# Layer 0's attention of a two-layer model: all engines in the order of the program text, with its pieces placed anew

## The chip, the cores and the metric

The kernel runs on one NeuronCore of a Trainium2 chip. A core has five engines with instruction streams of their own: TensorE (PE: matrix products, into PSUM), VectorE (DVE), ScalarE (ACT), GpSimd (POOL) and SyncE (SP, which here only issues DMAs). An engine works its instructions off in the order in which they were built into its stream, and waits at semaphores for the others. The metric is the device time of one execution in microseconds (us); smaller is better. Of a kernel the median of several executions is given; one more execution is recorded by the profiler.

## What is computed

Input are 8 batches of 512 tokens with 512 features. Four blocks follow each other, each with a residual and a layer norm behind it: attention with 16 heads, a mixture of 8 experts of which each token takes two, a second attention, and a feed-forward layer with integer weights. The change concerns the first attention and the router behind it:

```python
x = _layernorm(x + _L0_attn_ref(x, ...))
x = _layernorm(x + _L0_ffn_ref(x, ...))
x = _layernorm(x + _L1_attn_ref(x, ...))
x = _layernorm(x + _L1_ffn_ref(x, ...))

def _L0_attn_ref(x, WQ_w, WQ_b, WK_w, WK_b, WV_w, WV_b, WO_w, WO_b):
    q = (x @ WQ_w.T + WQ_b).reshape(b, s, NH, HD).transpose(0, 2, 1, 3)    # k and v likewise
    scores = jnp.einsum('bhqd,bhkd->bhqk', q, k) * (1.0 / math.sqrt(HD))
    scores = jnp.where(causal, -jnp.inf, scores)
    attn = jax.nn.softmax(scores, axis=-1)
    out = jnp.einsum('bhqk,bhkd->bhqd', attn, v)
    return out.transpose(0, 2, 1, 3).reshape(b, s, h) @ WO_w.T + WO_b

# in _L0_ffn_ref, the choice of the experts
router_logits = xf @ gate_weight.T + xf @ gate_delta.T
probs = jax.nn.softmax(router_logits.astype(jnp.float32), axis=-1)
routing_weights, selected = jax.lax.top_k(probs, TOP_K)
```

## The kernel before

`attention0` works batch by batch (b = 0 to 7). A batch has four groups g of four heads each, and a group three units u. A unit holds one or two tiles of 128 keys: `UNITS = ((0,), (1, 3), (2,))`; because of the causal mask a tile of keys meets only the queries from it on, so that the units are 512, 384 + 128 and 256 queries wide. The text below writes (g,u) for a place in this order.

In each place `scores` computes the products of keys and queries for the four heads on TensorE into the one score buffer of PSUM (`sc`), ACT takes the exponential into `p`, and POOL sets what the mask forbids to zero. Then the thunks follow that `plan` has put at this place, and then `product`, for the unit before: the weighted sum of the values on TensorE (`av`), and on DVE the addition of `p` to the group's total. In a group's second unit `normalise` follows for the group before: TensorE sums the total over the keys (`rs`), ACT copies the sums, DVE takes the reciprocal and multiplies `av` with it into `aoT`, and POOL adds the reciprocals to a watch (`g_total`), from which the kernel tells at its end whether the numbers stayed in range.

The thunks are: the values, queries and keys of this and the next group (`value`, `query`, `key`); and for the batch before: `project` (the output projection of one of four token tiles, with the residual added on DVE; the last one calls `layernorm`, which computes statistics on DVE and the root on POOL, scales the four tiles on DVE and writes them to DRAM by four DMAs of SP's queue), `turn` (transposes of one of four feature tiles on TensorE, copied from PSUM in turns by DVE and ACT), `score` (the router's logits), and `choose` (which sorts out the two experts of each token in about 24 small DVE operations and one of ACT). For the batch before that: `dispatch` (ranks within the experts), `one_hot` (24 DVE operations) and `enter` (16 products into a table). Finally `merge` folds one low-rank correction into an expert's weights: two small products, two copies on ACT, two additions on POOL.

The products of all thunks, of `rs` and of `merge` go through two PSUM buffers (`mm`, tag "mm"); a product can start when an earlier one has left its buffer. `aoT` has one buffer, which the four projections of a batch read and `normalise` of the next batch writes anew. `xs` has two buffers, `p` has two for the first unit and one for each other.

What sets the order: up to the first batch's first place, and from group 2 of the last batch on, `in_order` holds TensorE to the order of the program text. All else, that is nearly the whole of the seven batches, and the other engines always, is put in order by a scheduler at build time. Its order is fixed in the built program. In the profile the four projections stand on TensorE in pairs and singles from (1,0) to (1,2), the four transposes in (2,1) and (2,2), in pieces between the products of `av`.

Of the kernel before, what the change touches and what calls it, by code (L numbers as in the profile page):

```python
# [18 lines left out]
P = 128  # L19
NB = 8  # L20
# [364 lines left out]
class Router:  # L385
# [76 lines left out]
    def choose(self, b, parts, ps):  # L462
# [17 lines left out]
        nc.scalar.activation(tmp, tmp, AF.Exp)  # L480
        nc.vector.tensor_reduce(red, tmp, AX.X, ALU.add)
# [640 lines left out]
def attention0(env, guard, keep, routes, experts, dram, p_mm, tiles_ctx):  # L1122
# [8 lines left out]
    with ExitStack() as phase:  # L1131
# [81 lines left out]
        def project(b, t):  # L1213
            ps = mm([P, D], "ps_o")
            for c in range(ND):
                nc.tensor.matmul(ps, lhsT=aoTs[b][:, c, ts(t, P)], rhs=wo[:, c, :], start=c == 0, stop=c == ND - 1)  # L1216
            nc.vector.tensor_tensor(xs[b][:, t, :], ps, xs[b][:, t, :], ALU.add)
            if t == NT - 1:
                env.layernorm(b, router.rows[S * b : S * (b + 1)])

        x1Ts, logits = {}, {}
# [17 lines left out]

        def choose(b):  # L1240
            router.choose(b, logits.pop(b), mm([P, NT, E], "ps_r"))
# [36 lines left out]
        def product(b, g, u, p, acc):  # L1278
# [6 lines left out]
            for kt in UNITS[u]:  # L1285
# [5 lines left out]
                at += w  # L1291
            at = 0
            for kt in UNITS[u]:
                w = S - P * kt
                if u:
                    nc.vector.tensor_tensor(total[:, :, P * kt :], total[:, :, P * kt :], p[:, :, at : at + w], ALU.add)  # L1296
                at += w

        def normalise(b, g, acc):
# [8 lines left out]
            guard.watch_inverses(r_inv)  # L1308

        merges = [(e, c) for e in range(0, E, 2) for c in range(UPS)]  # L1310
# [7 lines left out]
        def plan(b):  # L1318
# [10 lines left out]
            if b:  # L1329
                places = ((1, 0), (1, 0), (1, 1), (1, 1) if last else (1, 2))  # L1330
                for t, slot in enumerate(places):
                    todo[slot].append(lambda t=t: project(pb, t))
                places = ((2, 0),) * 4 if last else ((2, 1), (2, 1), (2, 2), (2, 2))
                for c, slot in enumerate(places):
                    todo[slot].append(lambda c=c: turn(pb, c))
                todo[(2, 1) if last else (3, 0)].append(lambda: score(pb))
                todo[(2, 2) if last else (3, 1)].append(lambda: choose(pb))
                if not last:
                    todo[2, 0].append(merge)
                    todo[3, 0].append(merge)  # L1340
            if b == 0:
                todo[1, 0].append(lambda: router.merge_lora(mm([P, ND, E], "ps_wr")))
            if b > 1:
                todo[0, 2].append(lambda: dispatch(b - 2))
                todo[1, 1].append(lambda: enter(one_hot(b - 2, range(NT))))
# [6 lines left out]

        tiles = Tiles(env, router, experts.w)
# [16 lines left out]
        begun.enter_context(in_order(tc))  # L1370
# [4 lines left out]
        for b in range(NB):  # L1375
            todo = plan(b)
            for g in range(ND):
                if g == 2:
                    if b + 1 < NB:
                        load_xT(b + 1)  # L1380

                    nc.gpsimd.tensor_tensor(xs[b], xs[b], row[:, 1:2, :].to_broadcast([P, NT, D]), ALU.add)
                if g == 3 and b + 1 < NB:
                    load_x(b + 1)
# [9 lines left out]
                for u in range(len(UNITS)):  # L1394
                    p = scores(b, g, u)
                    for thunk in todo[g, u]:
                        thunk()
                    begun.close()
                    if waiting is not None:
                        waiting()  # L1400
                    if u == 1 and summing is not None:
                        summing()
                    waiting = lambda b=b, g=g, u=u, p=p, acc=acc: product(b, g, u, p, acc)
                summing = lambda b=b, g=g, acc=acc: normalise(b, g, acc)
        waiting()
        merge(2)
        summing()
# [622 lines left out]
```

## Time and profile before

| what | us |
|---|---|
| median of 3 runs | 2297.6 |
| lowest and highest of them | 2297.3, 2299.71 |
| the profiled execution, whole | 2295.71 |
| its span, first to last instruction | 2293.9 |
| TensorE busy in the span | 2240.5 |
| DVE, ACT, POOL busy in the span | 1245.0, 648.2, 501.6 |
| start of the third value tile of batch 1 | 92.42 |
| the same in batch 2 | 183.74 |
| the same in batch 7 | 650.06 |

The mean granted clock of TensorE is 0.994 of full speed. Layer 0's attention takes about the first 720 us of the span. "Busy" is the union of an engine's records. Matmuls overlap each other and their ends are modelled, so that a busy TensorE can also be one that waits between two of them. TensorE's waits in the first 740 us, as far as the profile shows them as idle time, are few:

```profile
PE sc L1264 <- ACT p L1268: 5.2, 7, 1.8
PE ps_q L1200 <- DMA experts<-in_xT: 4.4, 1, 4.4
PE ps_v L1193 <- DVE v L1195: 2.4, 4, 1.0
```

In such a line the instruction that waited stands first, behind the arrow the one that released it, then the total, the number of waits and the longest.

### The profile page before, as it was taken

The numbers are of one execution on the slowest core, as the hardware profiler recorded it, in microseconds if no ns is written. First come the engines' busy times: TensorE is split into PE (matmuls) and PEld (weight loads), VectorE is DVE, ScalarE is ACT, GpSimd is POOL, SyncE is SP. The second block draws the span as 40 slices with busy tenths as digits, with TensorE's granted clock in tenths as the row PEclk, the third lists the DMA queues.
The fourth block names the chain that finished last, engine by engine and source line by source line (L and its number), as shares of the span: only waits on it lengthen the run. The fifth ranks groups of instructions, "written<-read, shape, count | busy, mean of one in ns | idle before, by whom it ended". The sixth has DMA issues, their size and how long they took to land.

```text
span 2293.9 us, 24187 instructions
## 1 busy us (share of the span) xinstructions
PE 2240.5 (98%) x9430; PEld 1154.8 (50%) x9430; DVE 1245.0 (54%) x1974; ACT 648.2 (28%) x937; POOL 501.6 (22%) x493
## 2 busy tenths in 40 slices
PE   9999999999999999999998999999998999999997
PEld 3344444444444444444443334443343878888876
DVE  3457575666668432242216877777667544444443
ACT  2332323323324221111223323333332322222222
POOL 2231323413224231131125122321211000000000
PEclk9999999999999999999999999999999999999999
DMA  8010110101112234332233011100100100000000
GB/s 289 19 56 1 55 33 23 56 7 49 54 38 84 92 115 146 93 120 91 87 127 94 10 55 56 55 29 17 37 1 23 42 19 19 19 19 19 19 19 20
DMA packets 58444, 126.63 MB, mean 55 GB/s; under 512 B 6210, under 2 KB 6210, under 8 KB 58322
## 3 DMA queue, kind: packets, MB, share of 16 engines
q1 hardware_dynamic: 47040, 89.32, 11.1%
q0 software_dynamic: 10560, 34.61, 5.2%
q8 instruction: 77, 1.26, 0.2%
q10 hardware_dynamic: 722, 1.07, 0.1%
q14 instruction: 45, 0.37, 0.1%
HBM read 89.59 MB, written 35.39 MB: 54 GB/s over the span
## 4 chain that ended last, share of the span: by engine, by line
PE 76%; issue 8%; DVE 7%; DMA 4%; POOL 4%; ACT 2%; POOLq 0%; SPq 0%; ACTq 0%; DVEq 0%
PE ps_f L1069 7%; PE ps_g L1055 6%; PE ps_u L1055 6%; PE ps_gu L845 5%; PE ps_o L1216 5%; PE ps_o L1551 5%; PE av L1601 5%; PE sc L1579 4%; PE ps_q L1503 4%; PE ps_q L1200 4%; PE ps_k L1208 4%; PE ps_v L1193 4%; PE av L1288 3%; PE sc L1264 3%; PE ps_y L862 2%
## 5 line engine op out<-in xcount | busy, mean ns | idle before, releaser
L845 PE MATMUL ps_gu<-experts,xrT 128*128 128x512 f32 (+1 forms) x520 | 248.6, 601 | 0.0
L1268 ACT ACTIVATE p<-sc 128x2048 f32<-128x2048 f32 (+1 forms) x96 | 152.9, 1593 | 189.0 <-PE sc L1264 182.1
L1273 POOL TENSOR_SCALAR_AFFINE_SELECT p<-p 128x512 f32<-128x512 f32 x128 | 92.1, 734 | 380.1 <-ACT p L1268 376.6
L1060 DVE SCALAR_TENSOR_TENSOR hT<-ps_u,vec,sg 128x512 f32<-128x512 f32 x88 | 65.8, 748 | 201.4 <-PE ps_u L1055 201.4
L1069 PE MATMUL ps_f<-ffn_w,h_half 128*128 128x512 f32 x672 | 169.4, 392 | 1.1 <-DVE h_half L1064 1.1
L934 POOL TENSOR_TENSOR g_total<-g_total,r_inv 128x512 f32<-128x512 f32 x64 | 89.7, 1402 | 361.4 <-DVE r_inv L1612 286.2
L1612 DVE RECIPROCAL r_inv<-r_inv 128x512 f32<-128x512 f32 x32 | 106.8, 3339 | 105.4 <-ACT r_inv L931 105.4
L1582 ACT ACTIVATE p<-sc 128x1024 f32<-128x1024 f32 x128 | 124.1, 1021 | 130.3 <-PE sc L1579 119.7
L1296 DVE TENSOR_TENSOR p<-p 128x1536 f32<-128x1536 f32 (+2 forms) x96 | 129.3, 1346 | 38.5 <-POOL p L1273 21.5
L1055 PE MATMUL ps_g<-x_high,ffn_w 128*128 128x512 f32 x352 | 141.5, 402 | 3.0 <-DVE x L1557 3.0
L1069 PEld LDWEIGHTS ps_f<-ffn_w,h_half 128*128 128x128 f32 x672 | 124.5, 188 | 33.7 <-DVE h_half L1064 7.2
L848 DVE TENSOR_TENSOR h<-ps_gu,h 128x256 f32<-128x256 f32 x67 | 28.4, 424 | 205.2 <-ACT h L847 205.2
L1055 PE MATMUL ps_g<-x_low,ffn_w 128*128 128x512 f32 x352 | 139.4, 396 | 0.0
L1055 PE MATMUL ps_u<-x_high,ffn_w 128*128 128x512 f32 x352 | 139.2, 395 | 0.0
L1055 PE MATMUL ps_u<-x_low,ffn_w 128*128 128x512 f32 x352 | 139.2, 395 | 0.0
L1579 PE MATMUL sc<-qT,kT 64*128 64x512 f32 x512 | 127.9, 618 | 1.0 <-ACT qT L1505 0.7
L862 PE MATMUL ps_y<-experts,hT 128*128 128x512 f32 (+1 forms) x272 | 127.9, 592 | 0.5 <-ACT hT L856 0.5
L1200 PE MATMUL ps_q<-experts 128*128 128x512 f32 x256 | 120.4, 611 | 4.4 <-DMA experts<-in_xT 4.4
L845 PEld LDWEIGHTS ps_gu<-experts,xrT 128*128 128x128 f32 x520 | 89.6, 192 | 68.0 <-issue 68.0
L1601 PE MATMUL av<-p,v 128*64 128x512 f32 x512 | 123.8, 605 | 0.0
L1193 PE MATMUL ps_v<-experts 128*128 128x512 f32 x256 | 116.3, 602 | 2.4 <-DVE v L1195 2.4
L1208 PE MATMUL ps_k<-experts 128*128 128x512 f32 x256 | 117.5, 602 | 0.2 <-ACT r_inv L931 0.2
(256 smaller groups left out, 3544.5 us busy)
## 6 DMA issues: line engine op xcount, KB each, us to landing
results<-y SPq DMA_DIRECT2D x68, 256.0 KB
x<-in_x SPq DMA_DIRECT2D x8, 1024.0 KB
experts<-in_gate_up SPq DMA_DIRECT2D x8, 1024.0 KB
rows<-x SPq DMA_DIRECT2D x32, 256.0 KB
x<-rows SPq DMA_DIRECT2D x8, 1024.0 KB
experts<-in_xT SPq DMA_DIRECT2D x7, 1024.0 KB
out<-x SPq DMA_DIRECT2D x28, 256.0 KB
ffn_i<-in_wq_ffn SPq DMA_DIRECT2D x11, 512.0 KB
```

The costliest lines, as they stand in the source:

```text
L845: mm = nc.tensor.matmul(ps, lhsT=xT[:, c, :], rhs=self.weights(i, c), start=c == 0, stop=c == ND - 1)
L862: self.nc.tensor.matmul(ps, lhsT=hT[:, c, :], rhs=self.weights(i, ND + c), start=c == 0, stop=c == self.NI - 1)
L1055: nc.tensor.matmul(ps, lhsT=w[:, ts(dc, P)], rhs=x[:, dc, :], start=(dc, i) == (0, 0), stop=(dc, i) == (ND - 1, 1))
L1069: self.nc.tensor.matmul(os[t], lhsT=h[:, ts(t, P)], rhs=self.weights(2 * NHID + c), start=(c, i) == (0, 0), stop=(c, i) == (NHID - 1, 1))
L1193: nc.tensor.matmul(ps, lhsT=xts[b][:, c, ts(t, P)], rhs=wv[:, c, :], start=c == 0, stop=c == ND - 1)
L1200: nc.tensor.matmul(ps, lhsT=wq[:, g, ts(c, P)], rhs=xts[b][:, c, :], start=c == 0, stop=c == ND - 1)
L1208: nc.tensor.matmul(ps, lhsT=wk[:, g, ts(c, P)], rhs=xts[b][:, c, :], start=c == 0, stop=c == ND - 1)
L1268: nc.scalar.activation(p, sc[:, :, :width], AF.Exp, scale=scale)
L1296: nc.vector.tensor_tensor(total[:, :, P * kt :], total[:, :, P * kt :], p[:, :, at : at + w], ALU.add)
L1579: nc.tensor.matmul(sc[:, j, :], lhsT=st["kT"][hs, ts(kt, P)], rhs=st["qT"][g][hs, :], start=True, stop=True)
L1582: nc.scalar.activation(p, sc, AF.Exp, scale=scale)
L1601: nc.tensor.matmul(st["av"][HD * j : HD * (j + 1), :], lhsT=st["v"][:, kt, HD * j : HD * (j + 1)], rhs=p[:, j, :], start=kt == 0, stop=kt ...
```

## The change

Three things change, for batches 0 to 6. The in-order stretch now starts at the same place, but covers DVE, ACT and POOL as well as TensorE, and lasts to the start of the last batch. The pieces of the batch before are placed anew: projections at (1,0), (1,1), (1,2) and (2,0), ahead of the other thunks there; the layer norm cut into statistics beside each projection and a scaling step `norm` at (2,2); all four transposes at (3,0), the logits at (3,1), the choice's first half at (3,2) and its second half at (0,0) of the next batch; the one-hots in two halves at (1,2) and (2,0), and their entry into the table at (2,2). The bias is added to `xs` in four pieces from (2,0) to (3,0), and the next batch's `x` is loaded at (3,1). And in every place the addition to the total is cut off from `product` and stands ahead of the thunks, as do the watches of the reciprocals.

Batch 7 keeps its places, except for the second half of batch 5's choice, the additions and the watches; its order is the scheduler's up to group 2, as before.

```diff
@@ class Router, choose
         nc.vector.tensor_tensor(tmp, ps, bc(red), ALU.subtract)
         nc.scalar.activation(tmp, tmp, AF.Exp)
+
+        yield
         nc.vector.tensor_reduce(red, tmp, AX.X, ALU.add)
@@ project
             nc.vector.tensor_tensor(xs[b][:, t, :], ps, xs[b][:, t, :], ALU.add)
+            if b >= NB - 2:
+                if t == NT - 1:
+                    env.layernorm(b, router.rows[S * b : S * (b + 1)])
+                return
+            if t == 0:
+                norms[b] = [small.tile([P, NT, n], F32, name=name) for n, name in ((6, "stats"), (2, "mv"), (1, "rstd"))]
+            stats, mv, rstd = norms[b]
+            nc.vector.bn_stats(out=stats[:, t, :], in_=xs[b][:, t, :])
+            nc.vector.bn_aggr(out=mv[:, t, :], in_=stats[:, t, :])
             if t == NT - 1:
-                env.layernorm(b, router.rows[S * b : S * (b + 1)])
-
+                nc.gpsimd.tensor_scalar(rstd[:, :, 0], mv[:, :, 1], LN_EPS, None, ALU.add)
+                nc.gpsimd.tensor_tensor(rstd[:, :, 0], rstd[:, :, 0], env.neg_half, ALU.pow)
+
+        def norm(b):
+            stats, mv, rstd = norms.pop(b)
+            for t in range(NT):
+                x = xs[b][:, t, :]
+                nc.vector.tensor_scalar(x, x, mv[:, t, 0:1], rstd[:, t, :], ALU.subtract, ALU.mult)
+                nc.sync.dma_start(out=router.rows[S * b + P * t : S * b + P * (t + 1)], in_=x)
...
+        def begin_choice(b):
+            choosing[b] = router.choose(b, logits.pop(b), mm([P, NT, E], "ps_r"))
+            next(choosing[b])
+
+        def end_choice(b):
+            next(choosing.pop(b), None)
@@ product, now without the additions
+
+        def add(u, p, acc):
+            total, _ = acc
             at = 0
             for kt in UNITS[u]:
                 w = S - P * kt
-                if u:
-                    nc.vector.tensor_tensor(total[:, :, P * kt :], total[:, :, P * kt :], p[:, :, at : at + w], ALU.add)
+                nc.vector.tensor_tensor(total[:, :, P * kt :], total[:, :, P * kt :], p[:, :, at : at + w], ALU.add)
                 at += w
@@ plan
             if b:
-                places = ((1, 0), (1, 0), (1, 1), (1, 1) if last else (1, 2))
+                places = ((1, 0), (1, 0), (1, 1), (1, 1)) if last else ((1, 0), (1, 1), (1, 2), (2, 0))
                 for t, slot in enumerate(places):
-                    todo[slot].append(lambda t=t: project(pb, t))
...
+                    todo[slot].insert(0, lambda t=t: project(pb, t)) if not last else todo[slot].append(lambda t=t: project(pb, t))
...
+            elif b:
+                todo[2, 2].insert(0, lambda: norm(pb))
+                todo[3, 0] += [lambda c=c: turn(pb, c) for c in range(ND)]
+                todo[3, 1].append(lambda: score(pb))
+                todo[3, 2].append(lambda: begin_choice(pb))
+                todo[2, 0].append(merge)
+                todo[3, 0].append(merge)
+
+            for t, slot in enumerate(((2, 0), (2, 1), (2, 2), (3, 0))):
+                todo[slot].append(lambda t=t: nc.gpsimd.tensor_tensor(xs[b][:, t, :], xs[b][:, t, :], row[:, 1, :], ALU.add))
+            if b + 1 < NB:
+
+                todo[3, 1].append(lambda: load_x(b + 1))
...
             if b > 1:
+                todo[0, 0].append(lambda: end_choice(b - 2))
                 todo[0, 2].append(lambda: dispatch(b - 2))
-                todo[1, 1].append(lambda: enter(one_hot(b - 2, range(NT))))
+                if last:
+                    todo[1, 1].append(lambda: enter(one_hot(b - 2, range(NT))))
+                else:
+                    todo[1, 2].append(lambda: one_hot(b - 2, (0, 1)))
+                    todo[2, 0].append(lambda: rows.append(one_hot(b - 2, (2, 3))))
+                    todo[2, 2].append(lambda: enter(rows.pop()))
@@ the loop
-        begun.enter_context(in_order(tc))
+        begun.enter_context(in_order(tc, mybir.EngineType.DVE, mybir.EngineType.Activation, mybir.EngineType.Pool))
         query(0, 0)
         key(0, 0)
...
         for b in range(NB):
+            if b == NB - 1:
+                begun.close()
...
                     p = scores(b, g, u)
+                    while watches:
+                        guard.watch_inverses(watches.pop())
+                    if waiting is not None and waiting[2]:
+                        add(*waiting[2:])
                     for thunk in todo[g, u]:
                         thunk()
-                    begun.close()
                     if waiting is not None:
-                        waiting()
+                        product(*waiting)
                     if u == 1 and summing is not None:
-                        summing()
-                    waiting = lambda b=b, g=g, u=u, p=p, acc=acc: product(b, g, u, p, acc)
-                summing = lambda b=b, g=g, acc=acc: normalise(b, g, acc)
+                        normalise(*summing)
+                    waiting = b, g, u, p, acc
+                summing = b, g, acc
```

## The prediction

> **What bounds the kernel now.** I read the table by stretches first, with one stretch for each batch of layer 0's attention from batch 1 on. Columns: length; busy time and instructions of TensorE (PE), its weight loads, DVE, ACT and POOL; granted clock; DMA share; GB/s.
>
> ```profile
> 361.00:454.00 93.00, 92.13 (x477) 39.41 (x476) 59.40 (x112) 28.14 (x32) 28.93 (x27) 1.00 0.10 35
> 454.00:548.00 94.00, 92.42 (x477) 39.72 (x478) 60.88 (x112) 28.30 (x33) 28.93 (x27) 1.00 0.10 34
> ```
>
> TensorE is busy 98% of a batch, at full clock; DVE is busy 59 to 61 of 93 us. Next, TensorE's timeline of batch 5.
>
> ```profile
> 506.34 3.60 PE L1216 MATMUL ps_o<-experts,aoT 128*128 128x512 f32 x8
> ...
> 514.00 1.15 PE L1264 MATMUL sc<-q,k 32*128 32x384 f32 x16 [0.57 <-ACT p L1268]
> 515.08 3.70 PE L1200 MATMUL ps_q<-experts 128*128 128x512 f32 x8
> 518.62 0.60 PE L1228 MATMUL ps_x1T<-ident,x 128*128 128x128 f32 x4
> 519.15 1.04 PE L1288 MATMUL av<-p,v 128*32 128x512 f32 x2
> 520.12 0.66 PE L1228 MATMUL ps_x1T<-ident,x 128*128 128x128 f32 x4
> 520.71 0.63 PE L1288 MATMUL av<-p,v 128*32 128x512 f32 x3
> ```
>
> Busy time hides waits here: two records of the av product take 1.04 us in line 519.15, eight of them in unbroken form take 0.88 (500.30 to 501.18). So I count by start to start of unbroken pieces: a tile of v, q, k or o 3.53 (16 a batch); scores of the three units 1.07, 1.08, 0.65; av 0.88, 1.00, 0.57; row sums 0.97 (all seven four times); rank 0.46, table 1.84, a turn 0.53 (4), logits 1.00, a merge's pair 0.96 (2), router 0.89. The sum is 89.6 us. The third v tile starts at 183.74 in batch 2 and at 650.06 in batch 7: 93.3 a batch. So 3.7 us a batch are waits and broken pieces, and about 22 over batches 1 to 6: all that a better order could win.
>
> Third, DVE's timeline of the same batch.
>
> ```profile
> 503.18 3.35 DVE L1306 RECIPROCAL r_inv<-r_inv 128x512 f32<-128x512 f32 x1
> 506.44 2.83 DVE L1296 TENSOR_TENSOR p<-p 128x512 f32<-128x512 f32 x2
> 509.97 0.69 DVE L1307 TENSOR_TENSOR aoT<-av,r_inv 128x512 f32<-128x512 f32 x1 [0.70 <-PE ps_o L1216]
> 510.58 0.68 DVE L1217 TENSOR_TENSOR x<-ps_o,x 128x512 f32<-128x512 f32 x1
> ```
>
> The first group's normalising product writes aoT, of which there is one buffer; so it waits for the last projection of the batch before (506.34 to 509.86 on TensorE). Here the wait costs little: adds are put in front of it, and it waits 0.70 us.
>
> **The change, part by part.** I write (g,u) for group g, unit u, and follow a batch from 2 to 6. Its program holds DVE, ACT and POOL to written order as well.
>
> *Gains.* TensorE's pieces stand unbroken: the 3.7 us go, as far as nothing new waits.
>
> *Products, adds, watches, the choice's second half.* The counts stay. The score sums' adds stand ahead of a unit's own DVE work, and what they wait for (POOL's masking of a unit earlier) is long done. The choice's 24 small operations take about 6 us in (0,0) (456.0 to 462.9 before, adds among them); TensorE meanwhile computes scores and two tiles, over 8 us, so nothing waits. In (0,2) the rank product needs the last v's eviction, behind an add of 2.23 us: 0.3. The four POOL adds of the bias (4.65 us as one) lie beside TensorE. DMA issues do not change in count; on SP's queue x's load moves from the start of group 3 to (3,1) and the norm's four row writes from (2,1) (514.26) to (2,2), and x is wanted first in the next batch's (2,0), 40 us later: nothing. Cover gone, the load's 7.5 us (528.72) would show.
>
> *First new stall, (1,1) to (2,0).* The fourth projection moves from (1,2) to (2,0), but the aoT product stands in (1,1), and it waits for that projection. DVE runs in order, so behind it stand the add of (1,2), the third projection's eviction, its statistics and half of the one-hots (12 operations, 2.4). DVE's reciprocal is over some 9 us before the projection; DVE stands still. When the projection ends, TensorE wants the merge's two PSUM tiles; the first takes the buffer of the third projection. DVE must do: the product 0.60, add 1.68 + 0.55, eviction 0.70, and two hand-overs of 0.1 to 0.15: 3.8 us of waiting. The second tile uses the first's buffer and waits for ACT's copy, 0.60 and two hand-overs: 0.8. Together 4.6.
>
> POOL's rstd (0.32 + 1.04) waits for the fourth projection's statistics; behind it queue the merge's adds (2.83), a bias add (1.2) and the masks of (2,1) (1.23), 6.6 us in all. DVE's add of (2,2) wants these masks some 7.7 us after the statistics (the other half of the one-hots, the query, reciprocal and product lie between): nothing, with 1 us to spare; without it the norm below is later by as much.
>
> *Second new stall, (3,0).* The norm's four operations now stand in (2,2) behind reciprocal, product and add; the transposes follow at once in (3,0). From the end of (2,1)'s row sums: reciprocal starts after 1.05 (49.58 to 50.63 in batch 0), then 3.26 + 0.60 + 2.23 + 4 × 1.03 = 11.3 us to the last norm. TensorE arrives after 0.65 + 3.53 + 1.84 + 1.00 + 1.07 = 8.1; three of four transposes of the first turn are hidden, so 2.9. The second turn's buffer is the table's, two DVE operations (0.46, 0.42) later: 0.7. The third waits for the first's copy, behind an add (1.15 + 0.68 after the table, less what TensorE did): 1.3. The merge waits for the third's copy beyond the fourth turn: 0.4. Together 5.3. The before kernel spread the turns over (2,1) and (2,2).
>
> A batch so becomes 89.6 + 0.3 + 4.6 + 5.3 = 99.8, or +6.5; five batches: +32.5. Batch 1 has no table and no one-hots: 87.3 of work; its second merge tile waits for the fourth projection's eviction (0.93 + 1.15 + 0.70 after the third's; 6.2 in all), and its transposes arrive 1.84 earlier (6.2 in all): 99.7 against 91.3 before (92.42 to 183.74), +8.4. In batch 0 nothing stands between the first unit's scores and the second's but an av of 0.57 (0.88 more once), while exp takes 1.88 and two hand-overs: 1.4 + 1.4 + 0.6 of waiting, less about 1.3 that the broken queries and a POOL wait cost before: +2.1. Stalls: +43.
>
> *The clock.* Each of these stretches leaves TensorE nearly empty for 5 to 8 us. The trace shows what follows. Columns: stretch, length, TensorE busy, clock, DMA.
>
> ```profile
> 1216.00:1218.00 2.00, 0.00 (x0) 1.00 0.00 0
> 1220.00:1222.00 2.00, 1.91 (x5) 0.50 0.03 8
> 1222.00:1224.00 2.00, 2.00 (x8) 0.65 0.00 0
> 1224.00:1226.00 2.00, 2.00 (x8) 1.00 0.00 0
> ```
>
> After a gap of 4.87 us (1215.22 to 1220.09) TensorE runs about 3.4 us at half clock, which loses 1.7 us of work. After one of 3.00 (1775.25) it drops too (0.56 at 1778 to 1780), and after 1.76 + 0.54 (0.50 at 722 to 724). The price is bounded below by 0 a stretch (work that waits anyway loses nothing) and above by two such periods, 3.4. I take 1.7, since both stretches hold more idle time than the three in the trace that tripped or come near the longest: 12 stretches in batches 1 to 6, +20.
>
> The Trainium skill ("TensorE: Matmul & The Clock Gate", Part 1) speaks against such an order: a whole idle window of about 3.4 us halves the clock until a busy window has passed. By that rule a gap of 3.8 us holds a free-running whole window only at times, so by an estimate from the page the first stretch would trip perhaps half the time, and the sum would be some 5 us less. The trace dropped after 1.76 + 0.54, so the sum stays with the trace.
>
> Sum: +43 + 20 = +63. The profiled execution's span of 2293.9 (run 2295.7) becomes 2357 (2359). Its run lies 1.9 below the median of 2297.6, so the median becomes 2361.
>
> **The rivals.**
> *Stalls alone, the clock holds.* The merges and turns inside the stretches may count as activity: 699 to 702 lost 0.44 + 0.94 without a drop. Against it: the three drops above. 2297.6 + 43 = 2341.
> *Worse.* POOL's watch and bias adds run beside DVE; the 1024-wide add took 2.10 instead of 1.21 beside POOL's watch (507.18), the 1536-wide 2.17 instead of 1.76 (543.99). In (3,0) that is 0.4 + 0.9, over six batches 8; and a second period of half clock at each stretch adds up to 20. 2361 + 8 + about 12 = 2381.
> *Faster.* If the aoT product found its buffer free and the norm came in time, all of the 22 us would be won: 2297.6 - 22 = 2276. For it speaks TensorE's broken timeline; against it the wait in the line at 509.97, and the written order behind it. This decides if the two stretches cost together under 3.7 us instead of 9.9.
> *The order is not kept,* and waits stay as they were: 2298. The built program's order of all engines is the written one up to batch 6, and TensorE's order from batch 7 on is that of before, so I give it little.
>
> **How the numbers follow.** Stalls and clock, 2361: 0.56. Stalls alone, 2341: 0.22. Worse, 2381: 0.14. Faster, 2276: 0.05. No change: 0.03. Low end: the stalls alone less 20% of their 43 us, 2333. High end: the worse case and a little, 2386; outside lie the faster and unchanged cases and the ends of the others, about 0.18. Within 0.2% (4.6 us, about what a measurement of this kernel can tell) lies only the last case: same 0.03, faster 0.05, slower 0.92.
>
> **What would show it.** In the changed profile, among TensorE's waits: the merge's lora tiles for DVE's eviction of ps_o, about 3.8 us each, six times; the transposes for the norm, about 3; the aoT product on DVE waiting for ps_o some 9 us. DVE's busy time should not change by more than a few us. A stretch of one batch should last 100 to 104 us; a clock of 0.97 or so in it shows the drops, 1.00 that there are none. The prediction is wrong if TensorE finds the merge's buffer free at the end of the fourth projection, if the norm ends before the table does, or if DVE's order turns out to differ; batches of 90 us would be the faster rival's.

## The result, and the profile after

The changed kernel takes 2397.3 us (median of four runs, 2395.7 to 2399.7) beside 2297.5 of the kernel before on the same chip: a ratio of 1.0439, 95% interval 1.0418 to 1.0461. The forecast was 2361 with a range to 2386: the direction was right, the size was not. The profiled execution has a span of 2393.6 us, 99.7 more than before.

First, where the time lies. Lines of the code are those of the changed kernel from here on (the aoT product is L1339, the fourth projection's matmuls L1218, its eviction L1219, the norm L1237, the turns L1248, the adds L1328, the merge's pair L751). Start to start of the first value tile, batches 2 to 6 now last 109.8, 109.4, 109.0, 109.4 and 109.3 us, where they lasted 92.8 to 93.9. Batch 1 lasts 17.3 more than before, batch 0 2.7 more, and what follows the start of batch 7 takes 1652.8 us against 1652.6. So the whole loss lies in batches 0 to 6. The stretches of two batches, in the columns of the prediction's first lines (length; TensorE, its weight loads, DVE, ACT, POOL; granted clock; DMA):

```profile
413.00:522.00 109.00, 100.05 (x480) 42.24 (x476) 63.09 (x112) 28.59 (x32) 27.86 (x30) 0.92 0.09 30
522.00:631.00 109.00, 100.41 (x479) 42.48 (x476) 62.70 (x112) 28.59 (x32) 27.86 (x30) 0.91 0.09 29
```

Two things changed at once. TensorE's busy share fell from 98 to 92%, that is 8.6 us of waits a batch. And its busy time rose by 8 us with the same instructions, because the granted clock fell from 1.00 to 0.91. DVE, ACT and POOL are busy as long as before, within 4 us.

What TensorE waited for in batches 0 to 6, up to 740 us (total, times, longest):

```profile
PE ps_lora L751 <- DVE x L1219: 23.7, 7, 3.8
PE ps_x1T L1248 <- DVE x L1237: 12.1, 11, 3.3
PE ps_rank L517 <- DVE v L1197: 4.6, 5, 0.9
...
PE ps_x1T L1248 <- DVE x1T L162: 4.1, 6, 1.0
PE ps_lora L751 <- ACT scaled L762: 3.7, 5, 0.7
```

These are the two stretches of the prediction by name: the merge's tile for the third projection's eviction, six times 3.85 us, and the transposes for the norm. DVE's side of the first one, in batch 5:

```profile
566.12 3.35 DVE L1338 RECIPROCAL r_inv<-r_inv 128x512 f32<-128x512 f32 x1 [1.85 <-ACT r_inv L933]
578.78 0.69 DVE L1339 TENSOR_TENSOR aoT<-av,r_inv 128x512 f32<-128x512 f32 x1 [9.31 <-PE ps_o L1218]
579.38 2.54 DVE L1328 TENSOR_TENSOR p<-p 128x1536 f32<-128x1536 f32 x2
581.85 0.69 DVE L1219 TENSOR_TENSOR x<-ps_o,x 128x512 f32<-128x512 f32 x1
```

DVE stands still for 9.31 us at the head of its queue, waiting for the fourth projection; then come, in order, the product, the add and the eviction that TensorE wants. This is the forecast's chain, at its forecast length (3.85 us against 3.8).

TensorE's timeline through both stretches shows what the forecast did not have:

```profile
575.04 3.70 PE L1218 MATMUL ps_o<-experts,aoT 128*128 128x512 f32 x8
582.59 2.07 PE L751 MATMUL ps_lora<-lora 16*128 16x512 f32 x2 [3.85 <-DVE x L1219]
585.40 2.07 PE L751 MATMUL ps_lora<-lora 16*128 16x512 f32 x2 [0.75 <-ACT scaled L762]
587.40 1.08 PE L1318 MATMUL av<-p,v 128*32 128x256 f32 x8
588.41 2.09 PE L1294 MATMUL sc<-q,k 32*128 32x384 f32 x16
...
605.70 1.24 PE L1248 MATMUL ps_x1T<-ident,x 128*128 128x128 f32 x3 [1.26 <-DVE x L1237]
607.43 0.33 PE L1248 MATMUL ps_x1T<-ident,x 128*128 128x128 f32 x1 [0.49 <-DVE x L1237]
608.22 1.11 PE L1248 MATMUL ps_x1T<-ident,x 128*128 128x128 f32 x4 [0.46 <-DVE r_table L560]
609.95 1.97 PE L1248 MATMUL ps_x1T<-ident,x 128*128 128x128 f32 x8 [0.62 <-DVE x1T L162]
611.85 2.81 PE L751 MATMUL ps_lora<-lora 16*128 16x512 f32 x4
```

Eight records of av with 256 columns take 1.08 us at 587.40 and 0.64 elsewhere (529.17); the scores of 384 columns 2.09 instead of 1.15. TensorE runs at half speed well after the wait is over. To see how long, I cut the time at the points where the clock changes (length, TensorE busy, clock, DMA):

```profile
577.53:580.94 3.41, 1.21 (x3) 1.00 0.00 0
580.94:584.36 3.42, 1.77 (x2) 0.50 0.00 0
584.36:587.77 3.41, 2.66 (x7) 0.50 0.01 2
587.77:591.18 3.41, 3.41 (x25) 0.50 0.00 0
591.18:594.59 3.41, 3.41 (x12) 1.00 0.00 0
```

and in the second stretch:

```profile
604.83:608.24 3.41, 1.34 (x5) 1.00 0.64 235
608.24:611.65 3.41, 2.79 (x12) 0.50 0.31 116
611.65:615.07 3.42, 3.42 (x14) 0.50 0.50 139
615.07:618.48 3.41, 3.41 (x25) 0.50 0.43 168
618.48:621.89 3.41, 3.41 (x12) 1.00 0.00 0
```

Each of these two periods of half clock lasts three windows of 3.41 us, 10.24 us, where the forecast had one. Over the whole attention there are 12 such periods, one for each stretch as forecast: ten of three windows, one of four (in batch 1) and one of two (in batch 4), together 122.9 us or 36 windows. Half of what TensorE was busy in them is work lost: 53.6 us (the forecast's term was 20). In the window from 611.65 TensorE was busy all of the time, and the clock stayed at half all the same.

### The profile page after: what moved, and what is told of

Its sections match the earlier page's. It is cut to its first block, busy times and chain, and to the rows that moved or that the text cites. A ratio compares the mean times of both kernels' runs of the same rounds, so it can differ in the third digit from the quotient of the medians.

```text
span 2393.6 us, 24209 instructions
## 1 busy us (share of the span) xinstructions
PE 2292.4 (96%) x9430; PEld 1171.2 (49%) x9430; DVE 1261.3 (53%) x1974; ACT 650.4 (27%) x937; POOL 499.9 (21%) x517
## 3 DMA queue, kind: packets, MB, share of 16 engines
q8 instruction: 77, 1.26, 0.2%
## 4 chain that ended last, share of the span: by engine, by line
PE 77%; DVE 9%; issue 7%; DMA 2%; POOL 2%; ACT 2%; POOLq 0%; DVEq 0%; ACTq 0%; SPq 0%
PE ps_f L1071 6%; PE ps_g L1057 6%; PE ps_u L1057 6%; PE ps_q L1202 5%; PE ps_gu L847 5%; PE ps_o L1218 5%; PE av L1653 5%; PE ps_o L1603 5%; PE sc L1631 4%; PE ps_q L1555 4%; PE ps_v L1195 4%; PE sc L1294 4%; PE av L1318 3%; PE ps_k L1210 3%; DVE p L1328 3%
## 5 line engine op out<-in xcount | busy, mean ns | idle before, releaser
L1303 POOL TENSOR_SCALAR_AFFINE_SELECT p<-p 128x512 f32<-128x512 f32 x128 | 85.0, 676 | 429.6 <-ACT p L1298 420.1
L1664 DVE RECIPROCAL r_inv<-r_inv 128x512 f32<-128x512 f32 x32 | 106.8, 3339 | 106.6 <-ACT r_inv L933 106.6
L936 POOL TENSOR_TENSOR g_total<-g_total,r_inv 128x512 f32<-128x512 f32 x64 | 82.4, 1287 | 350.8 <-DVE r_inv L1664 287.4
L1328 DVE TENSOR_TENSOR p<-p 128x1536 f32<-128x1536 f32 (+2 forms) x96 | 137.2, 1429 | 5.1 <-PE av L1318 1.9
L1338 DVE RECIPROCAL r_inv<-r_inv 128x512 f32<-128x512 f32 x32 | 107.3, 3352 | 56.0 <-ACT r_inv L933 55.9
L1555 PE MATMUL ps_q<-hT,attn_qkv 128*128 128x512 f32 x256 | 117.6, 602 | 0.0
```

The source lines that it names most:

```text
L1555: nc.tensor.matmul(ps, lhsT=w_qkv[:, c, ts(g, P)], rhs=hT[:, c, :], start=c == 0, stop=c == ND - 1)
```

## The experiments

Fourteen kernels, each against the kernel before on the same chip (1.00 is the kernel before). "Half" is the sum of half-clock windows up to 760 us, worked out as above. In the faster runs this takes in the start of batch 7: of the sums of runs 5 and 7 to 14 some 4 to 14 us lie there, as do the 6.8 of the kernel before.

| run | what it is | us | ratio, 95% interval | half, us | work lost, us |
|---|---|---|---|---|---|
| before | the kernel before | 2297.5 | 1 | 6.8 | 3.3 |
| after | the change | 2397.3 | 1.0439 (1.0418 to 1.0461) | 122.9 | 53.6 |
| 1 | projections early | 2355.7 | 1.0258 (1.0221 to 1.0295) | 61.4 | 28.5 |
| 2 | norm early | 2373.2 | 1.0334 (1.0312 to 1.0357) | 71.7 | 32.1 |
| 3 | both | 2348.2 | 1.0225 (1.0208 to 1.0243) | 41.0 | 20.3 |
| 4 | 128-row merge | 2380.9 | 1.0368 (1.0346 to 1.0390) | 85.3 | 35.4 |
| 5 | only TensorE in order | 2313.9 | 1.0073 (1.0050 to 1.0095) | 35.3 | 17.3 |
| 6 | before, all in order | 2396.4 | 1.0430 (1.0401 to 1.0460) | 95.6 | 29.2 |
| 7 | all in order, spread | 2327.3 | 1.0130 (1.0101 to 1.0158) | 54.6 | 27.1 |
| 8 | 7, merge in (3,2) | 2339.6 | 1.0183 (1.0161 to 1.0204) | 44.4 | 19.3 |
| 9 | TensorE in order, turns spread | 2313.3 | 1.0076 (1.0049 to 1.0103) | 23.2 | 11.4 |
| 10 | all in order, turns spread | 2317.2 | 1.0098 (1.0071 to 1.0126) | 34.1 | 17.0 |
| 11 | only DVE free | 2313.2 | 1.0081 (1.0053 to 1.0109) | 33.6 | 16.4 |
| 12 | 9, choice earlier | 2303.2 | 1.0025 (1.0016 to 1.0034) | 17.1 | 8.5 |
| 13 | 12, choice earlier still | 2311.7 | 1.0070 (1.0054 to 1.0086) | 23.9 | 11.2 |
| 14 | 7 with 128-row merge | 2313.8 | 1.0073 (1.0055 to 1.0091) | 17.1 | 7.5 |

### Runs 1 to 3: each stretch taken away

Run 1:

```diff
-                places = ((1, 0), (1, 0), (1, 1), (1, 1)) if last else ((1, 0), (1, 1), (1, 2), (2, 0))
+                places = ((1, 0), (1, 0), (1, 1), (1, 1)) if last else ((1, 0), (1, 0), (1, 1), (1, 1))
-                for t, slot in enumerate(places):
+                for t, slot in reversed(list(enumerate(places))) if not last else enumerate(places):
```

> Here all four projections stand in (1,0) and (1,1), two in each, so the fourth is over before the first group's normalising product; nothing else differs from the changed kernel. Theory (a stretch costs its idle time and then three windows of 3.41 us at half clock): the first stretch goes in batches 1 to 6 with 3.85 + 0.75 us of waits and the 3.2 to 4.4 us of work that the half clock lost there (23.5 in all), so 51 us less: about 2346, one period of half clock a batch left, of about 10.2 us. Rival A (the waits alone matter, the clock's share lies elsewhere): 28 less, 2370. Rival B (the wait moves: some other DVE work becomes late for TensorE in (1,0) to (2,0)): no more than 15 less.

Run 2:

```diff
-                todo[2, 2].insert(0, lambda: norm(pb))
+                todo[2, 1].insert(0, lambda: norm(pb))
```

> The norm moves from the front of (2,2) to the front of (2,1), ahead of that unit's reciprocal; the fourth projection stays in (2,0). Theory: the transposes of (3,0) find their rows ready, the waits for the norm (about 1.8 a batch) go, those for the table's eviction and for x1T's copy (1.1) may stay; if the idle time left is too short to halve the clock, the period of half clock at (3,0) goes too (29.9 in all): 40 to 45 us less, about 2355. Rival A (the short waits that are left still halve the clock): 11 less, 2386. Rival B (the norm's four operations make DVE late for the next thing in (2,1) or (2,2)): unchanged, 2397, or more.

Run 3 has both edits.

> Both edits of the two kernels before. Theory: both stretches go; the clock stays at 1.00 through batches 1 to 6; of the 109.4 us of a batch 8.6 and about 7 go, 93 to 94 are left, and the time is 2298 to 2310, about that of the kernel before; if the broken pieces of the kernel before are also won, as much as 2280. Rival (one of the waits only moves): 2340 or more.

Run 1 came 41.6 us below the changed kernel (its two times are 2349.8, which is the profiled one, and 2361.7). The merge's 3.85 us are gone from the waits and the six periods at (2,0) with them, worth more than the 28 of waits alone (rival A). But 9 us of the forecast 51 did not come. That is less than the two times lie apart, but the trace shows that rival B has a part in it: TensorE's row sums now wait 2.7 us in each of five batches for a score sum's add. One-hots stand in front of that add on DVE, and TensorE, no longer held up before them, arrives while they run.

Run 2 came 24 us below, between the theory (40 to 45) and rival A (11). The waits for the norm are gone; the period at (3,0) stayed in batch 1, vanished in 2 and 3 and is one window in 4 to 6. But a new wait of up to 1.7 us for the query's eviction (behind the norm) appeared in five batches, 6.4 us in all, as rival B had it, and that for the copies of the turns rose from 4.1 to 9.1. The first stretch, which the edit leaves as it was, halved the clock for three windows in batches 1 to 3 and for two in batches 4 to 6: where the windows happen to begin also decides how many of them a gap costs.

Run 3 is the telling miss: 2348, the rival's side, not 2300. Both stretches are gone, and batches 2 to 6 still last 102.4 us each. From 458 to 562 us of run 3, a batch and a little more:

```profile
PE ps_k L1210 <- DVE q L1204: 6.0, 2, 3.0
PE rs L1335 <- DVE p L1328: 2.7, 1, 2.7
PE ps_rank L517 <- DVE v L1197: 0.9, 1, 0.9
```

The first two of these waits are not among the changed kernel's. DVE's timeline of run 3 shows the first one's making: twelve one-hots (from 453.30) and the norm (455.61, 1.91 us) stand ahead of the query's eviction at 457.44, for which TensorE's key tile waited 3.0 us. Moving one thing in a strictly ordered queue makes the next thing late.

### Runs 5, 6 and 11: whose order is it

Run 5, and run 11 with Activation and Pool kept in the list:

```diff
-        begun.enter_context(in_order(tc, mybir.EngineType.DVE, mybir.EngineType.Activation, mybir.EngineType.Pool))
+        begun.enter_context(in_order(tc))
```

> The changed kernel's places and steps, with TensorE alone held to the written order; DVE, ACT and POOL are ordered by the scheduler again. In the program so built TensorE's instructions stand exactly as in the changed kernel; on DVE the adds and the third projection's eviction stand ahead of the first group's normalising product, and the norm stands right behind the fourth projection's statistics, in (2,0). Theory (both stretches come from DVE's written order, and the half clock from the stretches): waits of 4.6 and 3 us and their 12 periods of half clock go, 2290, between 2275 and 2310, a clock of 1.00 in most of batches 2 to 6. Rival (the new places or TensorE's unbroken order cost by themselves, whatever DVE does): 2340 or more.

> The changed kernel with its places; only DVE is ordered by the scheduler again, TensorE, ACT and POOL stay in written order. Theory (the stretches are DVE's doing alone): as with all three free, 2314 within 8. Rival (POOL's written order, in which rstd stands behind the masks, or ACT's, makes up a part): 2335 or more.

Run 6 is the other half of the change: the kernel before, its places and steps unchanged, with all four engines in written order up to the last batch.

> The kernel before, places and all, with TensorE, DVE, ACT and POOL held to written order in batches 0 to 6. Theory (the written order puts DVE's work late where a wait stands at the head of its queue): the product still stands ahead of the fourth projection's eviction and now the whole norm and the adds stand behind it; slower than before by 2 to 5%, 2340 to 2400, with periods of half clock in each batch. Rival (only the moves of the fourth projection, the norm and the turns hurt, the written order alone wins the broken pieces): 2275 to 2300.

Run 5 came 4 us above its theory's range, and of batches 1 to 6 only 4 and 6 kept the full clock; runs 6 and 11 came out inside theirs. On the cause the three agree. With the changed kernel's places, and TensorE's instructions in exactly its order, freeing the other three engines brings 2313.9, and freeing DVE alone brings the same 2313.2: ACT's and POOL's written order costs nothing that can be measured. The written order on the old places costs 2396.4, as much as the whole change. So, at the new places, 83 of the 100 us are DVE's written order, and the places and steps with TensorE's order cost the other 16. Of these 16 some 14 are the half clock again (17.3 us of lost work in run 5, 3.3 in the kernel before). A reader of run 6 finds other waits than in the changed kernel, but the same kind:

```profile
PE ps_x1T L1228 <- DVE x L153: 25.8, 24, 2.1
PE ps_x1T L1228 <- DVE q L1202: 23.5, 6, 3.9
PE ps_table L556 <- DVE one_hot L547: 17.4, 40, 1.4
```

Run 5 also shows whether unbroken pieces win anything. Its batches without any half clock, 4 and 6 (all engines, as above):

```profile
371.50:464.60 93.10, 91.97 (x480) 39.09 (x476) 56.80 (x109) 28.52 (x32) 27.51 (x29) 1.00 0.10 35
562.70:655.90 93.20, 92.07 (x481) 39.15 (x477) 55.65 (x108) 28.52 (x32) 27.53 (x29) 1.00 0.12 34
```

TensorE's pieces are unbroken there, its waits are 1.1 us, and a batch lasts 93.2 us: what it lasted before. The 3.7 us a batch that the forecast booked as won are not there.

### Runs 4 and 14: what holds the clock down

```diff
     def merge(self, e, c, ps, scaled, factors=None):
...
-            self.delta(ps[i], e + i, c)
+            if factors:
+                self.nc.tensor.matmul(ps[i], lhsT=factors[0], rhs=factors[1], start=True, stop=True)
+            else:
+                self.delta(ps[i], e + i, c)
```

with factors = (wo[:, 0, :P], wo[:, 0, :]) in all 24 merges, twelve in batches 1 to 6 and twelve between 820 and 950 us: 128 rows instead of 16, the same 512 columns. The kernel so leaves out the low-rank corrections. Run 4 does this to the changed kernel, run 14 to run 7.

> The changed kernel, with the merge's matmuls of the low-rank factors (16 rows x 512) replaced by matmuls of the same size in columns with 128 rows (a tile of the output projection's weights by itself): as long, as many, same waits. It leaves out the factors, so the experts' weights of the first two groups come out as others. Theory A (a window counts as busy by how much of the array works, and 16 rows of 128 count for little, so that the merge's pairs hold the clock down): the period of half clock at (3,0) lasts two windows (6.8 us) instead of three, that of (2,0) two or three; 1.7 us less for each window, 10 to 20 us less in all: 2377 to 2387. Theory B (only idle time counts, any matmul is work): periods as long as before, 2397 within 3.

TensorE's waits in run 4 are those of the changed kernel (24.1 us for the eviction, 12.1 for the norm, 3.7 for ACT's copy), and yet the time is 16.4 us less; in the profiled executions 13.6 us of the gain lie in batches 0 to 6 and 2.1 behind them. The half-clock windows fell from 36 to 25, the lost work from 53.6 to 35.4. That is theory A's number, and it prices the clock apart from the waits. The second stretch lost windows in every batch (19 in all to 11), the first only some (17 to 14). The second stretch of run 4 in batch 5, cut where the clock changes:

```profile
593.65:597.07 3.42, 1.90 (x11) 1.00 0.65 251
597.07:600.48 3.41, 2.00 (x8) 0.50 0.72 264
600.48:603.89 3.41, 3.41 (x11) 0.50 0.17 27
603.89:607.31 3.42, 3.42 (x29) 1.00 0.76 284
```

The third window holds the last transposes (1.5 us) and the merge (1.9 us) and nothing idle, and after it the clock is back. In batch 4 of run 4 the windows begin at nearly the same point of the stretch as in the changed kernel's batch 5:

```profile
491.26:494.67 3.41, 2.72 (x12) 0.50 0.33 125
494.67:498.09 3.42, 3.42 (x5) 0.50 0.45 147
498.09:501.50 3.41, 3.41 (x29) 1.00 0.41 160
```

The first of these, with twelve records of transposes, is the changed kernel's window at 608.24; the second, a transpose and then the merge, is the one at 611.65. There the clock stayed at half, here it came back, so it is not only a matter of where the windows begin. In the first stretch the rows alone are not enough: run 4's window from 467.36, with the second pair of the merge in it, was busy for 2.67 of 3.42 us, like the one at 584.36, and both stayed at half. There the second wait (0.75 us) has its part. In run 7 a window with the same contents, transposes 1.3 and a 16-row merge 2.1, does not bring it back, nor does the next:

```profile
547.71:551.12 3.41, 1.58 (x14) 1.00 0.21 79
551.12:554.54 3.42, 3.42 (x12) 0.50 0.02 8
554.54:557.95 3.41, 3.41 (x25) 0.50 0.79 299
557.95:561.36 3.41, 3.41 (x12) 0.50 0.00 0
```

So a window in which TensorE's records leave no gap is not always a busy one to the clock: with 16 rows of 128 it stayed at half, with 128 rows it rose. That the clock weighs rows is what fits; the runs show only these two sizes. It fits the drops too, here in run 5 and then in run 3:

```profile
519.86:523.28 3.42, 3.09 (x17) 1.00 0.00 0
523.28:526.69 3.41, 3.41 (x18) 0.50 0.00 0
```

```profile
452.30:455.72 3.42, 1.71 (x16) 1.00 0.00 0
455.72:459.13 3.41, 0.89 (x2) 1.00 0.63 235
```

The window of run 5 is busy for 3.09 us, of which the two 16-row pairs of a merge fill 2.2, and the clock drops behind it. The first window of run 3 is busy for 1.71 us with row sums and scores alone, and the clock stays.

> The seventh run's places (the one with two projections each in (1,0) and (1,1), one-hots there, the norm in (2,0), all engines in written order; 2327), with the merge's 16-row matmuls replaced by 128-row ones as in the fourth run. It leaves out the factors. In batches 4 to 6 of the seventh run the clock is halved for three windows although TensorE is never idle in them. Theory A (rows count): the periods shrink to one window or none, of 27 us of lost work 12 to 20 go, about 2310. Theory B (only idle time or the transposes count): the periods stay, 2327 within 4.

Run 14 came 13.5 us below run 7, with the half-clock periods of batches 3 to 6 gone altogether. That is on theory A's side, but it says less than run 4: the windows of a run lie on a fixed grid (below), and in run 14 a line of the grid (546.39) falls into the second of the two waits at the turns (to 545.41 and to 547.14), which lie in one window in run 7. A part of the gain can be that, and 3.6 us of it lie behind batch 6.

### Runs 7 to 10, 12 and 13: a better order

Run 7:

```diff
...              (the places of the projections as in run 1)
-                    todo[1, 2].append(lambda: one_hot(b - 2, (0, 1)))
-                    todo[2, 0].append(lambda: rows.append(one_hot(b - 2, (2, 3))))
+                    todo[1, 0].append(lambda: one_hot(b - 2, (0, 1)))
+                    todo[1, 1].append(lambda: rows.append(one_hot(b - 2, (2, 3))))
-                todo[2, 2].insert(0, lambda: norm(pb))
+                todo[2, 0].append(lambda: norm(pb))
```

> All engines in written order; as in the third run two projections each in (1,0) and (1,1), and besides, the two halves of the one-hots in (1,0) and (1,1), where DVE stood idle, and the norm at the end of (2,0). Theory: of the waits of the third run those of the row sums for the score sums' add (2.7 a batch) and of the key for the query's eviction (3.0) go, with the period of half clock behind them (1.7); the small waits and the period of half clock at the turns and the merge in (3,0) stay (1.7): 7.4 less in each of five batches, about 2311. Rival (the norm in (2,0) makes the row sums wait as the one-hots did): 2325 to 2345.

Run 8 is run 7 with the second merge moved:

```diff
-                todo[3, 0].append(merge)
+                todo[3, 2].append(merge)
```

> As the kernel before it in this set, with the merge of (3,0) moved to (3,2), away from the turns. Theory (a window of transposes and 16-row matmuls counts as idle, even with little idle time in it): without the merge the windows at (3,0) hold enough full matmuls, the last period of half clock goes, 1.7 a batch: 10 less than the kernel with the merge in (3,0), about 2300. Rival (idle time alone decides): the same as that kernel, within 3.

Run 7's waits came out as expected (row sums gone, the key's at 0.2), but it took 2327 instead of 2311: the period at the turns grew from one window to three in batches 4 to 6, 98.9 us a batch, for the reason seen above. Run 8 was a miss: the merge in (3,2) meets the choice's PSUM tile and waits for DVE's reading of it, 14.0 us in six batches. Its time can't test what it was made for. In its trace the period at the turns is gone in batches 2 to 6, as its theory has it, but there too a line of the grid (560.15) falls between the two waits at the turns (to 559.75 and to 561.48), so that the merge need not be the reason.

Runs 9 and 10 take run 7's places, the table to (1,2) and the turns away from the merge; run 9 with TensorE alone in order, run 10 with all engines. The lines are those of run 9; in run 10 the turns stand in (2,1), (2,2), (2,2) and (3,0):

```diff
-                todo[3, 0] += [lambda c=c: turn(pb, c) for c in range(ND)]
+                for c, slot in enumerate(((2, 1), (2, 1), (2, 2), (2, 2))):
+                    todo[slot].append(lambda c=c: turn(pb, c))
-                    todo[2, 2].append(lambda: enter(rows.pop()))
+                    todo[1, 2].append(lambda: enter(rows.pop()))
```

> TensorE alone in written order, DVE, ACT and POOL ordered by the scheduler, as in the fifth run; besides, two projections each in (1,0) and (1,1), the one-hots there too, the table in (1,2), the norm in (2,0), two turns each in (2,1) and (2,2), each pair behind eight or more full matmuls; merges stay in (2,0) and (3,0). Theory (windows with many transposes and 16-row matmuls halve the clock, and the fifth run's 17.3 us of work lost to it is all that keeps it above the kernel before): at most two periods of half clock are left, 2285 to 2300. Rival (the turns now wait for PSUM buffers in (2,1) and (2,2) as the kernel before did): 2305 to 2320.

> All engines in written order, projections, one-hots, table and norm as in the run beside it, the turns one in (2,1), two in (2,2), one in (3,0). Theory: the two stretches are gone and the turns no longer stand beside the merge, so the 27 us of work that the fourth set of places lost to the half clock go for the most part: 2300 to 2312. Rival (DVE's written order makes the turns' copies wait behind reciprocal and adds, and TensorE with them): 2330 or more.

Run 9 missed its theory: the periods at the turns are gone, but the second value tile now waits 2.3 to 2.6 us for DVE to read the choice's tile, which the scheduler put behind the reciprocal, and one window at half clock follows in most batches. Run 10 came out 5 us above its theory's range, and 80 us below the changed kernel with all four engines in written order as well. So it is not the written order as such that costs 83 us, but the places that stood in it.

Run 12 is run 9 with the logits moved to the front of (3,1) and the choice's product to its end (the lines below). Run 13 puts the logits at the end of (3,0) and the whole choice, no longer cut in two, at the front of (3,1), and holds TensorE to the written order from batch 1 on only:

```diff
-                todo[3, 1].append(lambda: score(pb))
-                todo[3, 2].append(lambda: begin_choice(pb))
+                todo[3, 1].insert(0, lambda: score(pb))
+                todo[3, 1].append(lambda: begin_choice(pb))
```

> As the ninth run (TensorE alone in written order, projections, one-hots, table, norm and turns moved), with the logits at the front of (3,1) and the router's product at its end, ahead of the row sums, instead of in (3,2). On DVE the two operations that read the product's PSUM tile then stand ahead of the add and the reciprocal. Theory (the ninth run's wait of the second value tile, 2.3 to 2.6 a batch, and the period of half clock behind it, 1.7, are all that lie between its 96 us a batch and 92): about 20 less than it, 2290 to 2296, at or a little under the kernel before. Rival (a batch's work in this order is no shorter than the 93.3 us of the kernel before, whatever waits): 2298 or more.

> As the twelfth run, with the logits at the end of (3,0), the whole choice at the front of (3,1), and TensorE's written order from batch 1 on only (batch 0 is the scheduler's, as before). Theory (the wait of the third value tile for the first's eviction, 1.4 to 1.8 a batch, goes, and batch 0 wins back its 2.7 us): 10 to 12 us less than 2303, 2290 to 2293, and a batch of 91.5 to 92. Rival (93 us is what a batch's TensorE work takes in any order): 2298 to 2301.

Run 12 is the best of all at 2303.2, and still 0.25% (0.16 to 0.34%) slower than the kernel before: the rival. Its batches 3 to 5 last 93.2, 93.9 and 92.9 us; it loses 2.7 us in batch 0 and about 2 each in batches 2 and 6 (95.7 and 95.4). Run 13 came out above both its theory and its rival, 8.6 us slower than run 12: the logits wait 1.4 us for ACT's copy of the merge, the key 1.5 for the query's eviction, and a window of half clock follows in most batches. No version beat the kernel before; the shortest of batches 2 to 6 in any of them lasts 92.9 us, in the kernel before 92.8.

## Why the prediction was wrong

Step by step, by its own terms, in us for one batch of 2 to 6 (after: batch 5, 522.11 to 631.52; its lost work is 3.92 + 4.81):

| term | predicted | measured | worked out |
|---|---|---|---|
| bare TensorE work | 89.6 | 92.1 | 100.82 busy less 8.73 lost to the clock |
| rank | 0.3 | 0.9 | wait for the value tile's eviction |
| first stretch | 4.6 | 4.6 | 3.85 + 0.75 |
| second stretch | 5.3 | 2.8 | 1.26 + 0.49 + 0.46 + 0.62; 0.8 more lies in the transposes' records |
| clock | 3.4 | 8.7 | 3.92 + 4.81 |
| batch | 103.2 | 109.4 | with 0.3 of small gaps |

*The step that failed is the clock term, "I take 1.7".* That each of the twelve stretches would trip the clock was right, twelve of twelve. Its price was mis-sized: 4.5 us of work on the mean (53.6 / 12) instead of 1.7, and the upper bound of 3.4 did not hold it either. Of the 36 us between forecast and result this is 33. The three cases in the trace of before, from which the price came, all had matmuls of mostly 128 rows behind the gap (av and row sums at 722, projections at 1776), and one window was enough there. The same trace held a drop that pointed to the merge, and that the prediction did not use: from 735.29 to 738.71 TensorE was busy for 2.91 of 3.42 us, 2.3 of them 16-row matmuls, and the next window ran at 0.50. Here the gap is followed by what waited for it: a merge of 16 rows and a second wait of 0.75 in the first stretch, transposes and a merge in the second. The first two windows after the drop mostly don't bring the clock back, so the period lasts three. Run 4 shows it with all waits left in place: other rows, 11 windows less, 16.4 us less. Run 4 still has 25 windows where 12 were booked; what is left for them is the second wait of the first stretch, the transposes' waits in the second, and where the windows begin, and no run takes these three apart. The prediction's side estimate, that by a whole-window rule half the first stretches would trip, was loose too: a gap of 3.85 us covers a window of 3.413 us whole in about one case of eight, and all six tripped.

*The first stretch* was right in cause, place and size; runs 1, 5 and 11 take it away. *The second* was right in cause: the last norm lands 3.0 us after the scores end (604.44 to 607.43; forecast 11.3 - 8.1 = 3.2), though its parts moved against each other: the four norm operations took 2.26 us, not 4 × 1.03, the add before them 4.00, not 2.23. Three transposes that land one by one fill 1.24 of these 3.0 us, so the profile books 1.75 as idle; the table and the copies behind cost 1.1 instead of 2.4. *The rank's wait* was three times its forecast, since the add in front of the eviction took 3.19 us (544.59) instead of 2.23.

*The gain of 3.7 us a batch* was not there. Start to start the unbroken pieces sum to about 92 in run 5, as busy time said before; what I had priced at its best are the merges above all (0.96 for one, but 1.86 at 638.92 in run 5). The lesson of the lines at 519.15, that busy time hides waits, was read too far. This was 15 us too hopeful over six batches, and the waits' 10 us too dark hid most of it; that the two nearly cancel was luck.

*The rivals.* Stalls alone fell with the first half-clock window. The worse case had a second period at each stretch, the right direction, at 2381 still too little; the contention that it counted on DVE shows in two adds (3.19 and 4.00 instead of 2.23 us), of which TensorE paid 0.6 a batch at the rank, while the norm gave the other back. The faster case fell at run 5 and again at run 12: even with the product's buffer free and the norm in time, nothing is won. The order was kept.

Open is how the clock weighs matmuls: only two row counts were tried. An estimate from the windows of all 16 traces from 100 to 760 us: count the time of a 16-row merge, from start to start, for an eighth (16 of 128 rows) and that of all other matmuls in full, transposes too. Then, at full clock, windows with less than 1.62 us drop, and at half clock those with less than 2.94 stay, with 26 exceptions among 3084 windows (123 drops, 121 that stayed). Busy time alone, with its own best thresholds, leaves 100. The thresholds are fitted to the same windows, and no run tests them apart. A second aoT buffer, the direct cure of the first stretch, was not tried; aoT takes 8 KB a partition.

## What to carry to other kernels

When a queue is put in written order, look for the instruction that waits longest at its head and ask what stands behind it that another engine wants; here taking away that one wait (run 1) won back 42 of the 100 us. Price a stall on TensorE by what comes behind it as well: few-row matmuls after a gap keep the half clock on for windows on end; with 128-row ones in their place a third of the lost work went (run 4). And before booking busy time as hidden waits, check the pieces' sum in an order that has none.

## What the runs showed of the hardware

All changes of the granted clock in one execution fall on one grid of 3.413 us, over its whole length: in the changed kernel at 144.04, 154.28, 167.93, 181.58, 253.26 and so on, up to 2386.59, which all leave the same rest of 0.67 to 0.68 us when divided by 3.4133; in run 7 the rest is 1.58, in run 4 3.15, in run 14 0.25. The Trainium skill ("TensorE: Matmul & The Clock Gate", Part 1) states such a free-running window of 3413 ns, and the traces agree. It also asks a whole idle window for the drop; here windows that were busy for 1.21, 1.34, 1.58, 1.90 and, in run 5, 3.09 of 3.41 us dropped, so the measurement decides against that part.

DVE's small operations took longer beside POOL's adds: the same one-hot of 128x128 took 0.31 us at 589.51 and 1.26 at 590.10, where POOL's two adds of the merge ran (589.97, 2.57 us).
